# A 64-row half-width product and two row transfers in place of a full restoring product, in a two-layer attention kernel

## The chip, the cores and the metric

The kernel runs on one core of a Trainium2 chip. The metric is the time on the device for one execution, in microseconds (us), given as the median over runs. In what follows PE is TensorE (matmuls; PEld is its weight load), DVE is VectorE, ACT is ScalarE, POOL is GpSimd, and SP is the engine that only issues transfers. POOL issues transfers too, from a queue of its own.

## The reference, cut to what matters

Two residual attention layers run over four images of 32x32 tokens with 768 channels (12 heads of 64). The second layer, called layer 1 in the code, computes a depthwise 3x3 convolution of q, k and v, normalises each head, and adds q itself to what attention gives:

```python
q, k, v = (qkv[0], qkv[1], qkv[2])
q = layer_norm(dwconv3x3(q, w_pool_q), g_q, b_q)
k = layer_norm(dwconv3x3(k, w_pool_k), g_k, b_k)
v = layer_norm(dwconv3x3(v, w_pool_v), g_v, b_v)
ori_q = q
attn = jnp.einsum('bqc,bkc->bqk', qf * scale, kf)
attn = attn.reshape(B * nh, H, W, H, W) + rel_h[:, :, :, :, None] + rel_w[:, :, :, None, :]
attn = jax.nn.softmax(attn.reshape(B * nh, H * W, H * W), axis=-1)
o = attn @ vf
o = o.reshape(B * nh, H, W, hd) + ori_q
return o @ w_proj.T + b_proj
```

Layer 0 is plain attention with the same kind of relative-position terms. Each layer is preceded by a group norm.

## The kernel before, in words

**Stages and pairs.** The work is 8 stages of one image and one layer each, in the order (0,L0) (1,L0) (0,L1) (1,L1) (2,L0) (3,L0) (2,L1) (3,L1). A stage is six pairs of heads (`hp` 0 to 5), so there are 48 pairs, and 24 of them belong to layer 1. The 128 partitions hold two heads of 64 channels.

**Sixteen steps for a pair.** `attend` takes a pair in two halves of 512 queries (`c`), and each half in two groups of four key tiles. A group is four times [scores L804, relative-position term L806, exponential L811], then two steps in which other work is emitted, then the product with v (`av`, L828), then two more such steps. The relative-position term is a matmul of `bias` by a table of zeros and ones, `ones`, which is filled at the start from the input `picks` by two transfers and one ACT cast (L369).

**The order is written out by hand.** For PE, DVE, ACT and POOL the program order is the order in which the Python code emits instructions. `Pair.plan` lists what is prepared for a pair and at which step; step 0 is the start of the attention of the pair before it, so step -8 lies in the middle of the pair before that. In layer 1 the list has, among others: the product for q, k or v with its copy into a padded image (`padded(s, h)`: 24 matmul instructions `qkv`, then ACT L527), the nine taps of the convolution on DVE (L542, L544), `centre` (PE transposes `ln_c` L556 in two halves; for each half a DVE reduction L559 and a subtraction L560), `norm` (DVE L582), and `back` (PE transposes `ln_t` L591, then ACT L495 and L496 that write `q` and `q_t`). Work emitted at one step for different pairs follows in the order of the list `events`. Step 8 of one pair and step -8 of the next one coincide, so `centre(K)` of pair i, `padded(Q, 0)` of pair i+1 and, a step later, `back(Q, ...)` of pair i stand one behind another.

**Banks.** Products that are not scores take the PSUM banks of two places, left and right, in a fixed rotation, `behind_scores` being left, left, right, right and `behind_av` right, right, a small bank, left, left. A product waits for whoever used its bank last.

**The replaced channel.** In layer 1 channel 63 of each head's v is overwritten with ones (L584), so that rows 63 and 127 of `av` come out as the softmax's sums. `copy` (inside `attend`) brings `av` to SBUF as `weighed` (ACT L741), and two POOL transfers spread the two rows over all partitions: `z<-weighed` (L747) and `t<-z` (L748). A few steps later `sums` runs: `restore` (L751 to L755) multiplies the whole of `weighed` by a 128x128 matrix in the constants, `WHOLE`, which keeps 63 channels of a head and rebuilds the 64th as minus their sum (a normalised head sums to zero), in two products of 64 output rows each; ACT L755 copies the 128x512 result back. ACT L768, L776 and L777 then take the reciprocal of the sums, and at a later step `result` finishes on DVE: L784, L785, the division L788 (`inv<-weighed,inv`) and the addition of q (L789). Of the 48 halves of layer 1, 47 go this way. The very last half sums with `acc` and a product `z` instead, and restores afterwards.

**The end.** `project` multiplies the six pairs' outputs by the projection weights in seven products for a pair of output tiles. `put` adds product, bias and the residual `x` (L900), then a second term (L902), and stores (L903).

Of the kernel before, what the change touches and what calls it, by code (L numbers as in the profile page):

```python
# [9 lines left out]
F32 = mybir.dt.float32  # L10
F32R = mybir.dt.float32r
I32 = mybir.dt.int32
AF = mybir.ActivationFunctionType
ALU = mybir.AluOpType
# [3 lines left out]
P = 128  # L18
B = 4
S = 32  # L20
T = S * S
C = 768
NC = C // P
D = 64
HALF = T // 2
QC = 512
# [11 lines left out]
IDENT, GROUP, CENTRE, HEADS, ONES, WHOLE = 0, P, 2 * P, 3 * P, 3 * P + 2, 3 * P + 2 + D  # L38
# [7 lines left out]
def two_layers(ctx: ExitStack, tc: tile.TileContext, keep, x_in, wqkv, wproj, rels, windows, vrow, small, const, onehot, picks, out):  # L46
# [19 lines left out]
    nc = tc.nc  # L66
    pool = lambda name, bufs, **kw: ctx.enter_context(tc.tile_pool(name=name, bufs=bufs, **kw))
    fixed = pool("fixed", 1)
# [4 lines left out]
    one = pool("one", 1)  # L73
# [67 lines left out]
    cst = fixed.tile([P, NCONST], F32, tag="cst", name="cst")  # L141
# [5 lines left out]
    def col(c, lo=0, hi=P):  # L147
        return sm[lo:hi, c : c + 1]
# [15 lines left out]
    stages = [(b0 + k, layer) for b0 in range(0, B, 2) for layer in range(2) for k in range(2)]  # L164
# [53 lines left out]
    for i, (_, layer, hp) in enumerate(items):  # L218
        first = (i - 1) * 16 + shift(i)
# [142 lines left out]

    pbias = fixed.tile([P, NC], F32, tag="pbias", name="pbias")

    ones = fixed.tile([P, T], F32R, tag="ones", name="ones")
    plain = one.tile([P, T], F32, tag="whole", name="plain")
    for j in range(2):
        nc.sync.dma_start(plain[j * D : (j + 1) * D, :], picks)
    nc.scalar.copy(ones, plain)  # L369
# [5 lines left out]
    class Pair:  # L375
# [267 lines left out]
        def plan(self):  # L643

            Q, K, V = 0, 1, 2
            if not self.layer and not in_sevens(self.i):
                return [
                    (0, lambda: self.plain(Q, 0)),
                    (2, lambda: self.plain(Q, 1)),
                    (4, lambda: self.plain(K, 0)),  # L650
                    (5, lambda: self.positions(0)),
                    (6, lambda: self.plain(K, 1)),
                    (7, lambda: self.positions(1)),
                    (8, lambda: self.split()),
                    (8, lambda: self.plain_v(0)),
                    (10, lambda: self.plain_v(1)),
                ]
            if not self.layer:
                pieces = [
                    (0, lambda: self.sevens(Q, False)),  # L660
                    (2, lambda: self.sevens(Q, True)),
                ]

                first = 4 if shift(self.i) else 6
                pieces += [
                    (first, lambda: self.positions(0)),
                    (first + 2, lambda: self.positions(1)),
                    (first + 4, lambda: self.split()),
                ]
                if self.hp % 2 == 0:  # L670
                    pieces += [(8, lambda: self.sevens(V, False)), (10, lambda: self.sevens(V, True))]
                return [(r + shift(self.i), piece) for r, piece in pieces]


            late = self.hp in (0, NC // 2)
            pieces = [
                (-8, lambda: self.padded(Q, 0)),
                (-6, lambda: self.padded(Q, 1)),
                (-4, lambda: self.padded(K, 0)),
                (-2, lambda: self.padded(K, 1)),  # L680
                (2, lambda: self.padded(V, 0)),
                (4, lambda: self.padded(V, 1)),
                (3, lambda: self.centre(Q)),
                (4, lambda: self.square(Q)),
                (6, lambda: self.squares(Q)),
                (8 if late else 7, lambda: self.norm(Q)),
                (8, lambda: self.centre(K)),
                (9, lambda: self.back(Q, 0)),
                (9, lambda: self.back(Q, 1)),
                (10, lambda: self.square(K)),  # L690
                (11, lambda: self.squares(K)),
                (10, lambda: self.positions(0)),
                (11, lambda: self.positions(1)),
                (12, lambda: self.norm(K)),
                (11 if short(self.i) and self.hp == NC - 1 else 12, lambda: self.split()),
                (13, lambda: self.centre(V)),
                (14, lambda: self.back(K, 0)),
                (14, lambda: self.back(K, 1)),
                (14, lambda: self.square(V)),
                (15, lambda: self.squares(V)),  # L700
                (15, lambda: self.norm(V)),
            ]

            taps = (
                (Q, -4, (2, 2, 2, 2, 1)),
                (K, 2, (2, 2, 2, 2, 1)),
                (V, 8, (2, 2, 3, 2)),
            )
            for s, r, counts in taps:
                lo = 0  # L710
                for n in counts:
                    pieces.append((r, lambda s=s, lo=lo, n=n: self.taps(s, lo, lo + n)))
                    r, lo = r + 1, lo + n
            return pieces
# [4 lines left out]
    def attend(pair, os):  # L719


        q, k, bias = pair.q, pair.k, pair.bias
# [12 lines left out]
        for c in range(T // QC):  # L735
            cols = slice(c * QC, (c + 1) * QC)
# [14 lines left out]
            def restore(weighed):  # L751

                ps = small_bank("whole")
                halves(ps, cst[:, WHOLE : WHOLE + P], weighed)
                nc.scalar.copy(weighed, ps)  # L755

            def landed(*found):

                return found

            def sums(weighed, of, c=c, ones=by_ones[c]):

                at = 2 * (pair.i * (T // QC) + c)
                inv = work.tile([P, QC], F32, tag="inv", name="inv", bufs=1)
                if ones:
                    t = of
                    restore(weighed)
                    nc.scalar.activation(inv, t, AF.Copy, accum_out=seen[:, at : at + 1])  # L768
                else:
                    z = small_bank("z")  # L770
                    t = work.tile([P, QC], F32, tag="t", name="t", bufs=1)
                    for j, rows in enumerate(heads):
                        nc.tensor.matmul(z[rows, :], cst[:, ONES : ONES + D], of[:, j, :], start=True, stop=True)  # L773
                    nc.scalar.activation(t, z, AF.Copy, accum_out=seen[:, at : at + 1])

                nc.scalar.activation(inv, t, AF.Ln, bias=tiny)  # L776
                nc.scalar.activation(inv, inv, AF.Exp, scale=-1.0, accum_out=seen[:, at + 1 : at + 2])  # L777
                if pair.layer and not ones:
                    restore(weighed)
                return weighed, t, inv  # L780
# [17 lines left out]
            for g in range(0, NKT, 4):  # L798
                es = []
                for kt, place in zip(range(g, g + 4), (None, place_b, place_c, None)):  # L800
                    keys = slice(kt * P, (kt + 1) * P)
                    ps = place.pair("s") if place else ps_a.tile([P, 2, 512], F32, tag="a", name="s")
                    for j, rows in enumerate(heads):
                        nc.tensor.matmul(ps[:, j, :], k[rows, keys], q[rows, cols], start=True, stop=False)  # L804
                    for j, rows in enumerate(heads):
                        nc.tensor.matmul(  # L806
                            ps[:, j, :], ones[rows, keys], bias[c][rows, kt // 2, :],
                            start=False, stop=True,
                        )
                    e = work.tile([P, 2, QC], F32, tag="e", name="e", bufs=4)  # L810
                    nc.scalar.activation(e, ps, AF.Exp)  # L811
                    es.append(e)
# [12 lines left out]
                for t, e in enumerate(es):  # L825
                    kt = g + t
                    for j in range(2):
                        nc.tensor.matmul(  # L828
                            av[j * D : (j + 1) * D, :], pair.vt[:, kt, j * D : (j + 1) * D], e[:, j, :],
                            start=(kt == 0), stop=(kt == NKT - 1),  # L830
# [11 lines left out]
    def project(stage, os):  # L842
# [52 lines left out]
            nc.sync.dma_start(x, src[:, which, cols])  # L895
            return x

        def put(which, cols, x, ps, term=None):
            bias = pbias[:, which : which + 1] if layer else col(BIAS[0] + 18 + which)
            nc.vector.scalar_tensor_tensor(x, ps, bias, x, ALU.add, ALU.add)  # L900
            if term is not None:
                nc.vector.tensor_tensor(x, x, term, ALU.add)  # L902
            nc.sync.dma_start(dst[:, which, cols], x)  # L903

        add = lambda to, x, y, op=ALU.add: nc.vector.tensor_tensor(to, x, y, op)
# [34 lines left out]
        def three(pair):  # L940
            u, w = extra(9), extra(10)
            b3, b4 = bank("p1p6"), bank("p7")
            x11, x22 = get(2 * pair, first), get(2 * pair + 1, second)
            m(b3, pair, 4, lambda n: extra(n + 6))
            add(u, u, b3)
            m(b4, pair, 5, lambda n: os[n + 3][:, first])
            load(4 * pair + 4)
            put(2 * pair, first, x11, b4, u)
            m(b3, pair, 6, lambda n: os[n][:, second], more=True)
            load(4 * pair + 5)  # L950
            put(2 * pair + 1, second, x22, b3, w)

        def products():
            for pair in range(NC // 2):
# [320 lines left out]
def _laid_out(inp):  # L1275
# [38 lines left out]
    for i in range(S // 2):  # L1314
# [10 lines left out]
        "small": np.ascontiguousarray(np.concatenate(cols, axis=1)),  # L1325
        "const": const,
        "onehot": onehot.astype(np.float32),
        "picks": picks.reshape(D, T),
    }


# [15 lines left out]
```

## Time and profile before

| | |
|---|---|
| runs before | 3830.72, 3829.58, 3828.72 us; median 3829.58 |
| span of the profiled execution | 3830.7 us |
| mean granted TensorE clock | 0.999 |
| busy: PE / PEld | 3767.9 us (98%) / 1642.7 us |
| busy: DVE / ACT / POOL | 2468.2 (64%) / 1793.7 (47%) / 478.1 us (12%) |
| layer 1's taps on DVE, L544 | 758.2 us in 576, 1316 ns each |
| restoring products on PE, `whole<-weighed,cst` | 192 instructions, 4 for each of 48 |
| their copies on ACT, L755 | 28.1 us in 48, 586 ns each |

The table is from the summary page and from the groups of instructions. Busy times of different engines overlap and can't be added. An fp32 matmul of the program appears as two instructions. In the groups, the mean of a PE instruction is from its issue to its end and several are under way at once, so its busy total divided by its count tells more about its price than the mean. No time is given for the profiled execution beside its span; the span equals the first run shown, 3830.72 us, to the last digit that it has, and nothing measurable lies around it.

### The profile page before, as it was taken

How to read it: one execution, taken by the hardware profiler on the slowest of the kernel's cores; microseconds unless marked ns; L12 is line 12 of the kernel's file. 1: busy time of each engine (PE TensorE's matmuls, PEld its weight loads, DVE VectorE, ACT ScalarE, POOL GpSimd, SP SyncE). 2: the span in 40 equal slices, each digit the busy share in tenths (PEclk: the TensorE clock that was granted, in tenths of full speed). 3: DMA queues.
4: the chain of work that ended last, by engine and by line, in shares of the span. 5: the costliest groups of instructions: out<-in, count | busy, mean ns of one | idle time of the engine just before them, and what ended most of it. 6: DMA issues, size and time to landing. Idle time of an engine off the chain costs nothing.

```text
span 3830.7 us, 76084 instructions
## 1 busy us (share of the span) xinstructions
PE 3767.9 (98%) x32990; PEld 1642.7 (43%) x32990; DVE 2468.2 (64%) x3068; ACT 1793.7 (47%) x2573; POOL 478.1 (12%) x870
## 2 busy tenths in 40 slices
PE   8999999999999999999999999999999999999998
PEld 4535535533344443444535445355333444434442
DVE  2566454559678877688454564455686887867774
ACT  3455434545345553455534554254442555534552
POOL 0111100111111211111200010011111111111120
PEclk9999999999999999999999999999999999999999
DMA  4344452331431223311333122522124222142123
GB/s 155 103 120 118 131 151 83 101 79 42 124 94 48 64 51 98 119 47 48 83 114 121 52 76 61 178 58 75 44 55 141 66 60 55 48 124 62 46 57 100
DMA packets 211014, 330.62 MB, mean 86 GB/s; under 512 B 47570, under 2 KB 100562, under 8 KB 210672
## 3 DMA queue, kind: packets, MB, share of 16 engines
q1 hardware_dynamic: 122912, 212.26, 17.7%
q0 software_dynamic: 87760, 113.40, 12.4%
q8 instruction: 263, 4.31, 0.5%
q14 instruction: 79, 0.65, 0.1%
HBM read 184.62 MB, written 40.10 MB: 59 GB/s over the span
## 4 chain that ended last, share of the span: by engine, by line
PE 90%; DVE 6%; ACT 2%; DMA 1%; issue 1%; SPq 0%; POOL 0%; DVEq 0%; ACTq 0%
PE qkv L131 19%; PE s L804 17%; PE av L828 16%; PE m4m L131 5%; PE m3m L131 4%; PE m1m L131 4%; PE s L806 4%; PE p3p L131 3%; PE p4p L131 3%; PE p1p L131 3%; PE rel L613 3%; PE m L131 2%; PE ln_c L556 2%; DVE shared L544 1%; PE z L773 1%; PE whole L131 1%
## 5 line engine op out<-in xcount | busy, mean ns | idle before, releaser
L811 ACT ACTIVATE e<-s 128x1024 f32<-128x1024 f32 x768 | 775.0, 1024 | 423.2 <-PE s L806 392.8
L131 PE MATMUL qkv<-xn,wqkv_t 128*64 128x512 f32 x3648 | 814.4, 595 | 4.8 <-DVE gmean L334 2.6
L804 PE MATMUL s<-q,k 64*128 64x512 f32 x3072 | 807.1, 602 | 5.0 <-ACT e L811 4.1
L544 DVE SCALAR_TENSOR_TENSOR shared<-shared,sm 128x1056 f32<-128x1056 f32 x576 | 758.2, 1316 | 15.6
L806 PE MATMUL s<-bias,ones 64*128 64x512 f32 x1536 | 610.9, 788 | 1.0 <-DMA bias<-whole 1.0
L828 PE MATMUL av<-e,vt 128*64 128x512 f32 x2624 | 595.7, 596 | 0.0
L640 POOL DMA_DIRECT2D bias<-high x384 | 205.6, 556 | 2180.4 <-ACT high L629 1943.3
L131 PEld LDWEIGHTS qkv<-xn,wqkv_t 128*64 128x64 f32 x3648 | 251.3, 137 | 492.7 <-issue 482.8
L822 DVE TENSOR_TENSOR acc<-acc,e 128x1024 f32<-128x1024 f32 x294 | 360.2, 1225 | 114.0 <-ACT e L811 87.4
L804 PEld LDWEIGHTS s<-q,k 64*128 64x128 f32 x3072 | 279.4, 186 | 261.9 <-issue 210.7
L527 ACT ACTIVATE shared<-qkv,sm 128x512 f32<-128x512 f32 (+1 forms) x288 | 129.1, 501 | 500.0 <-PE qkv L131 500.0
L828 PEld LDWEIGHTS av<-e,vt 128*64 128x64 f32 x2624 | 181.3, 137 | 350.0 <-issue 315.4
L806 PEld LDWEIGHTS s<-bias,ones 64*128 64x128 f32 x1536 | 148.7, 187 | 184.2 <-issue 182.7
L640 POOL DMA_DIRECT2D bias<-whole x384 | 207.2, 571 | 55.7 <-DVE whole L630 46.7
L820 DVE TENSOR_TENSOR acc<-e 128x1024 f32<-128x1024 f32 x49 | 60.0, 1225 | 215.3 <-ACT e L811 206.7
L741 ACT COPY weighed<-av 128x512 f32<-128x512 f32 x96 | 56.3, 586 | 278.6 <-PE av L828 265.0
L559 DVE TENSOR_REDUCE mean<-ln_c 128x8 f32<-128x512 f32 x144 | 98.7, 686 | 114.5 <-PE ln_c L556 114.5
L613 PEld LDWEIGHTS rel<-q,rel 64*32 64x32 f32 x6144 | 111.8, 105 | 78.4 <-issue 73.5
L747 POOL DMA_DIRECT2D z<-weighed x47 | 27.2, 578 | 881.7 <-ACT weighed L741 476.3
L613 PE MATMUL rel<-q_t,rel 64*32 64x32 f32 x6144 | 123.4, 195 | 2.5 <-issue 2.5
L570 DVE TENSOR_REDUCE lnv<-shared 128x16 f32<-128x1024 f32 x72 | 87.5, 1216 | 58.2 <-ACT shared L566 58.2
L613 PE MATMUL rel<-q,rel 64*32 64x32 f32 x6144 | 122.4, 195 | 2.3 <-issue 2.3
(158 smaller groups left out, 4394.6 us busy)
## 6 DMA issues: line engine op xcount, KB each, us to landing
bias<-high POOLq DMA_DIRECT2D x384, 128.0 KB, 2.9
bias<-whole POOLq DMA_DIRECT2D x384, 128.0 KB, 3.0
wqkv_t<-in_wqkv SPq DMA_DIRECT2D x78, 384.0 KB, 3.2
wqkv_t<-mixed SPq DMA_DIRECT2D x66, 384.0 KB, 3.1
wproj_t<-mixed SPq DMA_DIRECT2D x48, 384.0 KB, 3.2
wqkv_t<-in_wqkv SPq DMA_DIRECT2D x66, 192.0 KB, 2.5
xn<-in_x SPq DMA_DIRECT2D x24, 512.0 KB, 8.8
x<-in_x SPq DMA_DIRECT2D x48, 256.0 KB, 3.3
```

What stands on the lines that cost most here:

```text
L131: nc.tensor.matmul(ps[lo : lo + D], a[:, lo : lo + D], b, start=start, stop=stop, **kw)
L527: nc.scalar.activation(self.pad[s][:, rows, there : there + src.shape[2]], src, AF.Identity, bias=col(self.column(s)))
L544: nc.vector.scalar_tensor_tensor(y, window, tap, y, ALU.mult, ALU.add)
L559: nc.vector.tensor_reduce(of, heads, AX.X, ALU.add)
L570: nc.vector.tensor_reduce(v, squared.rearrange("p (a d) -> p a d", d=D), AX.X, ALU.add)
L613: nc.tensor.matmul(ps[lo : lo + S, k * S : (k + 1) * S].rearrange("p (b c) -> p b c", b=2), rel[rows, 2 * self.layer + i, first : first + ...
L640: nc.gpsimd.dma_start(sets, some.unsqueeze(1).to_broadcast([D // 2, 2, QC]))
L804: nc.tensor.matmul(ps[:, j, :], k[rows, keys], q[rows, cols], start=True, stop=False)
L806: nc.tensor.matmul(ps[:, j, :], ones[rows, keys], bias[c][rows, kt // 2, :], start=False, stop=True,)
L811: nc.scalar.activation(e, ps, AF.Exp)
L822: nc.vector.tensor_tensor(acc, acc, e, ALU.add)
L828: nc.tensor.matmul(av[j * D : (j + 1) * D, :], pair.vt[:, kt, j * D : (j + 1) * D], e[:, j, :], start=(kt == 0), stop=(kt == NKT - 1),)
```

## The change

Four things are changed.

1. In the 47 halves that go by ones, `restore_last` replaces `restore`. Its weights are the odd columns of `WHOLE` (64 columns at a stride of two), whose last one of each 32 is the rebuilt channel of a head. Two products take 256 of the 512 columns each and land on the two halves of the partitions of one bank. ACT copies 128x256 to a new tile `last`, and two POOL transfers carry two rows of 256 values each into rows 63 and 127 of `weighed`.
2. `padded(Q, 0)` goes from step -8 to step -7, except for `hp` 1 and 4: the 24 instructions of the product, and its ACT copies, stand behind `back(Q, 0)` and `back(Q, 1)` of the pair before instead of ahead of them.
3. The table `ones` is 128x256 instead of 128x1024, and its input and load shrink with it; the four key tiles read the same two tiles of it in turn.
4. The last stage's last pair of output tiles adds the second term to `x` ahead of the product instead of behind it.

```diff
-    ones = fixed.tile([P, T], F32R, tag="ones", name="ones")
-    plain = one.tile([P, T], F32, tag="whole", name="plain")
+    ones = fixed.tile([P, 2 * P], F32R, tag="ones", name="ones")
+    plain = one.tile([P, 2 * P], F32, tag="whole", name="plain")
...
+            early_late = self.hp in (1, NC // 2 + 1)
             pieces = [
-                (-8, lambda: self.padded(Q, 0)),
+                (-8 if early_late else -7, lambda: self.padded(Q, 0)),
...
+            def restore_last(weighed):
+
+                ps = small_bank("last")
+                odd = cst[:, WHOLE + 1 : WHOLE + P : 2]
+                for h in range(2):
+                    nc.tensor.matmul(
+                        ps[h * D : (h + 1) * D, : QC // 2], odd, weighed[:, h * (QC // 2) : (h + 1) * (QC // 2)],
+                        start=True, stop=True,
+                    )
+                last = one.tile([P, QC // 2], F32, tag="last", name="last")
+                nc.scalar.copy(last, ps[:, : QC // 2])
+                for h in range(2):
+                    rows = last[h * D + D // 2 - 1 : (h + 1) * D : D // 2, :]
+                    nc.gpsimd.dma_start(weighed[D - 1 :: D, h * (QC // 2) : (h + 1) * (QC // 2)], rows)
...
                 if ones:
                     t = of
-                    restore(weighed)
+                    restore_last(weighed)
...
-                            ps[:, j, :], ones[rows, keys], bias[c][rows, kt // 2, :],
+                            ps[:, j, :], ones[rows, kt % 2 * P : (kt % 2 + 1) * P], bias[c][rows, kt // 2, :],
...
-        def put(which, cols, x, ps, term=None):
+        def put(which, cols, x, ps, term=None, term_first=False):
...
+            if term is not None and term_first:
+                add(x, x, term)
             nc.vector.scalar_tensor_tensor(x, ps, bias, x, ALU.add, ALU.add)
-            if term is not None:
-                nc.vector.tensor_tensor(x, x, term, ALU.add)
+            if term is not None and not term_first:
+                add(x, x, term)
...
+            last = stage == stages[-1] and pair == NC // 2 - 1
-            put(2 * pair, first, x11, b4, u)
+            put(2 * pair, first, x11, b4, u, last)
-            put(2 * pair + 1, second, x22, b3, w)
+            put(2 * pair + 1, second, x22, b3, w, last)
...
-        "picks": picks.reshape(D, T),
+        "picks": np.ascontiguousarray(picks.reshape(D, T)[:, : 2 * P]),
```

## The prediction

> **What bounds the kernel now.** I read the summary page first.
>
> ```profile
> PE 3767.9 (98%) x32990; PEld 1642.7 (43%) x32990; DVE 2468.2 (64%) x3068; ACT 1793.7 (47%) x2573; POOL 478.1 (12%) x870
> PE 90%; DVE 6%; ACT 2%; DMA 1%; issue 1%; SPq 0%; POOL 0%; DVEq 0%; ACTq 0%
> ```
>
> The first line is busy time by engine, the second the chain that ended last, by engine. PE is busy for 98% and is 90% of the chain; all its gaps make 63 us. So a PE instruction that goes is worth its time if nothing late stands just behind it. Next the groups of instructions, for the operations that the change touches:
>
> ```profile
> L131 PE MATMUL whole<-weighed,cst 128*64 128x512 f32 x192 | 50.0, 599 | 2.0 <-ACT t L774 2.0
> L131 PE MATMUL m3m<-wqkv_t,xn 128*64 128x128 f32 x1056 | 62.0, 273 | 0.0
> L755 ACT COPY weighed<-whole 128x512 f32<-128x512 f32 x48 | 28.1, 586 | 169.3 <-PE whole L131 167.4 <-issue 1.9
> L747 POOL DMA_DIRECT2D z<-weighed x47 | 27.2, 578 | 881.7 <-ACT weighed L741 476.3 <-ACT ln_ln L153 309.6 <-ACT ln_gn L153 95.8
> ```
>
> Here the restoring product is 192 instructions, four for each half. The second row is another product with 64 columns of weights that moves 128 columns. On the timeline, four `whole` instructions take 0.858 us from start to the next instruction's start where a product follows: 0.2145 each.
>
> For the moved product I read PE's and DVE's timelines, at one of its two places where the norm comes late:
>
> ```profile
> 1451.54 1.09 PE L556 MATMUL ln_c<-cst,shared 128*128 128x128 f32 x8
> 1452.56 5.37 PE L131 MATMUL qkv<-xn,wqkv_t 128*64 128x512 f32 x24
> 1457.86 1.09 PE L591 MATMUL ln_t<-cst,shared 128*128 128x128 f32 x8
> ```
>
> ```profile
> 1451.95 1.22 DVE L582 TENSOR_TENSOR shared<-shared,r_ln 128x1024 f32<-128x1024 f32 x1
> 1453.09 0.68 DVE L559 TENSOR_REDUCE mean<-ln_c 128x8 f32<-128x512 f32 x1
> 1453.81 0.69 DVE L560 SCALAR_TENSOR_TENSOR shared<-mean,ln_c 128x512 f32<-128x512 f32 x1
> ```
>
> The columns are start and duration. `ln_t` reads what L582 writes (it ends at 1453.17), so today the product's 5.3 us cover that wait. For the start I read the chain of its first 40 us:
>
> ```profile
> 8.20 9.70 DMA plain<-in_picks
> ...
> 17.99 1.04 ACT ones L369
> 19.03 0.11 ACT ln_gn L153
> ```
>
> The table's load and cast stand ahead of the group norm on the path to the first product.
>
> **What the Trainium skill says.** "TensorE: Matmul & The Clock Gate", section "Wait — 56ns, not 53.3ns?", gives columns / 2.4 GHz plus 2.5 ns for a matmul; the trace agrees (0.2145 us at 512; 62.0/1056 = 0.0587 at 128). "SBUF — State Buffer", section "Specifications (TRN2)", has cachelines of 16 bytes that want two hits for full bandwidth; weights at a stride of two fp32 have two. No row of before shows strided weights. "DMA: Bandwidth & Descriptors", "Anatomy of one DMA — SWDGE (gpsimd) path", prices a POOL transfer at about 2.0 us fixed; the trace has a median of 1.7 us from issue to landing for `z<-weighed`, 4 KB. "SBUF — State Buffer", "SBUF: two separate sides", warns that some DVE operations lock POOL out of writing descriptors; this trace suggests it (POOL L748 starts up to 2.75 us late behind a DVE L886).
>
> **The change part by part.**
>
> *The shorter product.* A new instruction moves 256 columns. Between 0.0587 at 128 and 0.2145 at 512, the line gives 0.111, so four take 0.443 and each restore gives back 0.858 - 0.443 = 0.415 us. 47 of them: -19.5. Two of the 47 (at 1813.9 and 3701.5) lie ahead of `rel` stretches where PE stalls by over 2 us anyway; I count those lost, with the like smaller cases: +0.8. Sum **-18.7**, between -17.5 (more of it lost in gaps) and -20.4. If strided weights loaded at half speed, four loads at twice the 0.056 us that 128-column products sustain would take 0.112 each, beside matmuls of 0.111: no cost.
>
> *The copy.* 128x256 for 128x512 saves about 0.25 us on ACT, which is idle ahead of it (169.3 us over 48): nothing, since neither ACT nor what follows it there is on the path, except at the end (below).
>
> *The two transfers.* Each of 47 restores adds two POOL issues at about 0.57 us (54 us on an engine 12% busy) and one wait: L788 on DVE now waits for their landing. From L755's end to L788's start the trace has 8.5 us at the least in the ordinary halves, 11.8 and 17.9 in others. Needed: 2 x 0.57 + 1.7 = 2.9 us. POOL's own `z`, `t` and bias issues then lie elsewhere; the nearest bias ones start over 3 us later. The transfers take the POOL queue's turn ahead of the bias transfers by 1.1 us, and those wait far longer for ACT's `high`. Behind L788 stand the taps, and behind these `ln_c` on PE, but with 5 us to spare the cost is 0. If the cover went, DVE's gaps of 2.9 to 6.6 us ahead of K's centre would take the first of it.
>
> *The end.* In the last pair's first half, L755 ends at 3754.09 and L788 starts at 3757.71: 3.6 us of cover against 2.9, and L788 is on the path there (L788, L741, L774, then PE after a gap of 1.96). The shorter product and copy bring up to -0.7; a late landing up to +1. I take **0**.
>
> *The moved product.* In 14 places it changes its order on PE (in the first layer-1 pair the order is the same). Before: `ln_c` 1.02, `qkv` 5.30, `ln_t` 1.02, no gap. After: `ln_c`, `ln_t`, `qkv`. Two waits appear. `ln_t` needs L582, which ends before `ln_t` can start in 12 places and 0.6 us after in two. And by the rotation of the banks the product takes the bank of the first half of `ln_c`, so it waits for the first L560, 2.11 us after `ln_c` starts (0.15 more to PE), when `ln_t` has ended at 1.9 to 2.0: 0.3 us. In rows without a product between them, `ln_c` plus `ln_t` take 1.90 instead of 2.04, so net I take 0.1 for 12 places (0 to 0.3), 0.95 for two (to 1.2): 1.2 + 1.9 = **+3.1**, between -1 and +6. Below nothing because ACT's `q` and `q_t` come 5 us earlier; but `q_t` ends 0.96 us ahead of the `rel` that reads it, and after 0.43 less of `restore` still 0.5 ahead, so I see no PE gap that this closes. What is late next is the product's copy, L527, and the taps come four steps later.
>
> *The narrow table.* 64 KB instead of 256 KB twice, and a cast of 0.35 instead of 1.04 us. The path then passes to the group's statistics, whose last DVE operation ends at 17.74; the logarithm could start about 17.9 instead of 19.03. **-1.15** (-1.5 to 0). The weights that the 1536 `bias` matmuls read from the table keep their shape: 0.
>
> *The last tiles.* The final L900 and L902 (0.75 and 0.69) follow the last product. With the addition put first, it must wait for its `x`, issued at 3820.23 and landed at 3823.3, just ahead of the product's end at 3823.5: **-0.2** (-0.7 to 0).
>
> Sum: -18.7 + 0 + 3.1 - 1.15 - 0.2 = -17.0 on 3830.7, 3813.7. The three runs' median stands 1.1 below the span: **3812.6**. All bounds together give 3806 to 3819.
>
> **The rivals.**
>
> *Waits take the gain's place (chance 0.12).* PE's queue is in order; if the moved product waited for both halves of `ln_c` (3.43 us after its start) or if DVE ran later than today, it would stall 1.5 us in 14 places, +21 instead of +3: 3830, no change. For it: `PE ln_t` already waits 6.1 us for L560 in seven places. Against: today's DVE order is kept, and the bank is the first half's. Half of it would give 3821.
>
> *The transfers land late (0.05), the other side.* The place is L788: the trace shows POOL held up by DVE, and the taps fill DVE at 1316 ns each, so descriptors could wait. Up to 8.5 us nothing happens; the next 2.9 us go into DVE's gap; from about 11.4 us each further us costs 47 on PE. It turns slower at 11.8 us; at 12.4 the bill is +47 - 17 = +30: 3860. Against: `z<-weighed` never took above 4.2 us to land, under the same taps.
>
> *The product doesn't get shorter (0.06).* If a strided load took 0.2 us, four times today's, it would replace the matmul as the limit and the first term would go: 3830.7 - 1.1 + 3.1 - 1.35, about 3831. Against: the two hits in a line above.
>
> **How the numbers follow.** The sum as worked out has 0.77. What a measurement here can tell from no change is 0.2%, 7.7 us. Its own range is 3806 to 3819; to hold 8 in 10 I stretch it to 3821 for a half-eaten gain. Faster by over 0.2%: 0.77 and some half of the first rival: 0.84. Within: the rest of it and the third, 0.11. Slower: 0.05.
>
> **What would show it.** Right: a row `last<-weighed,cst` of 188 instructions at some 21 us busy; PE busy down by 19 to 21 us; `ln_c`, `ln_t`, `qkv` with gaps of 0.3 us ahead of `qkv`; L788 (now L804) never released by a DMA except perhaps in the last pair; the first product about 1.1 us earlier. Wrong: waits of DVE for `weighed` by DMA, gaps over 1 us ahead of the moved product, or a `last` row with over 30 us.

## The result, and the profile after

The changed kernel takes 3815.74 us (median of 4 runs, 3814.61 to 3816.65) against 3830.15 before: a ratio of 0.9959, interval 0.9945 to 0.9973. Two repeats beside other experiments gave 3814.64 against 3831.85 (0.9956, 0.9943 to 0.9970) and 3814.63 against 3831.83 (0.9953, 0.9939 to 0.9967). So the change saves between 14 and 17 us, 0.4 to 0.5%; -17.0 was forecast, and 3812.6 for the median, 3.1 below the first of these results. The profiled execution's span went from 3830.7 to 3814.6, by 16.1.

One reading ahead of the change was wrong at the outset: something does lie around the span. The profiled execution of after lasted 3816.61 us with a span of 3814.6, so some 2.0 us. A span of before of 3830.7 then stands for an estimated 3832.7, which is above its median and not equal to its first run. Changes of spans are therefore compared with each other below, and medians with medians.

The summary page of after, busy time by engine:

```profile
PE 3749.5 (98%) x32990; PEld 1656.7 (43%) x32990; DVE 2467.1 (65%) x3068; ACT 1786.5 (47%) x2573; POOL 529.1 (14%) x964
```

PE lost 18.4 us of busy time and is still the bound; POOL gained 51 us for 94 more instructions. The groups of instructions of after, for the new operations (busy time, mean ns of one, then idle time before them):

```profile
L763 PE MATMUL last<-weighed,cst 128*64 128x256 f32 x188 | 28.9, 381 | 0.0
L768 ACT COPY last<-last 128x256 f32<-128x256 f32 x47 | 17.5, 372 | 175.8 <-PE last L763 175.8
L771 POOL DMA_DIRECT2D weighed<-last x94 | 50.7, 541 | 679.6 <-ACT last L768 638.6 <-DVE shared L544 38.1 <-issue 2.9
```

In the busy total of a PE group each run of instructions counts its last one to its modelled end, after the next product has begun, so the price is read from starts: on the timeline, four `last` instructions take 0.431 us to the next product's start, where four `whole` took 0.858. One place on PE's timeline, of before and then of after:

```profile
1205.65 1.03 PE L131 MATMUL whole<-weighed,cst 128*64 128x512 f32 x4
1206.51 5.32 PE L131 MATMUL qkv<-xn,wqkv_t 128*64 128x512 f32 x24
```

```profile
1204.75 0.60 PE L763 MATMUL last<-weighed,cst 128*64 128x256 f32 x4
1205.18 5.32 PE L131 MATMUL qkv<-xn,wqkv_t 128*64 128x512 f32 x24
```

The saving is 0.427 for each restore.

Where the time went is seen by subtracting, for the same exponential on ACT, its start in the two timelines. The difference is nearly a staircase: it falls by 0.36 to 0.45, mostly 0.43, for one restore after the other through layer 1, stage after stage, with few exceptions. The main ones are the start (-0.37 at the first exponential), a rise by 1.7 near 915 us, a rise by 0.84 above the expected step near 1450 and 3340 us, a rise by 2.9 near 1815 us, and the end, where it goes from -14.0 to -16.1. The experiments were chosen for these.

PE's timeline at one of the two late places of the move, to be held against the lines of the same place before:

```profile
1447.64 1.09 PE L556 MATMUL ln_c<-cst,shared 128*128 128x128 f32 x8
1449.41 1.06 PE L591 MATMUL ln_t<-cst,shared 128*128 128x128 f32 x8 [0.67 <-DVE shared L582]
1450.68 5.37 PE L131 MATMUL qkv<-xn,wqkv_t 128*64 128x512 f32 x24 [0.21 <-PE ln_t L591]
```

and at one of the twelve ordinary ones:

```profile
1082.93 1.09 PE L556 MATMUL ln_c<-cst,shared 128*128 128x128 f32 x8
1083.86 1.04 PE L591 MATMUL ln_t<-cst,shared 128*128 128x128 f32 x8
1085.18 5.37 PE L131 MATMUL qkv<-xn,wqkv_t 128*64 128x512 f32 x24 [0.28 <-DVE shared L560]
```

The bracket is PE's idle time ahead and what ended it. The two forecast waits are there: `ln_t` for the norm L582 (0.67), and the product for the first L560 (0.28). From `ln_c` to the instruction behind the three groups the ordinary places take 7.38 to 7.43 us, where they took 7.34 to 7.35; the late ones take 8.21.

At the start, ACT's timeline has the cast of the table at 16.36, 0.41 us long, while the statistics still run, instead of between them and the logarithm. But the last DVE statistics of `xn` now start at 15.02 instead of 14.22, waiting for their load, so the first product starts at 20.68 instead of 21.05: 0.37 earlier. At the end, DVE's timeline has

```profile
3807.40 0.69 DVE L923 TENSOR_TENSOR x<-x,os_sums 128x512 f32<-128x512 f32 x1 [1.91 <-DMA x<-mid]
3808.20 0.75 DVE L918 SCALAR_TENSOR_TENSOR x<-p1p,pbias,x 128x512 f32<-128x512 f32 x1
```

so the last addition (L923, moved ahead) waits for the load of its `x`. From the start of the last product's group to the end of DVE it is 4.55 us against 4.28 before. Of the kernels below, e13 has the new order too and takes 4.25, and e10 has the old one and takes 4.63, so no difference between the orders is shown.

The rise near 1815 us is the one that nothing in the prediction named. ACT's timeline of after there:

```profile
1808.14 0.37 ACT L768 COPY last<-last 128x256 f32<-128x256 f32 x1 [0.85 <-PE last L763]
1811.12 0.63 ACT L784 ACTIVATE inv<-t 128x512 f32<-128x512 f32 x1 [2.61 <-DMA t<-z]
...
1814.21 0.56 ACT L618 COPY whole<-rel 64x512 f32<-64x512 f32 x1
1814.78 1.01 ACT L619 COPY whole<-rel 64x512 f32<-64x512 f32 x1
```

and of before:

```profile
1815.01 0.59 ACT L755 COPY weighed<-whole 128x512 f32<-128x512 f32 x1 [1.28 <-PE whole L131]
1815.49 0.63 ACT L768 ACTIVATE inv<-t 128x512 f32<-128x512 f32 x1
```

Before, the activation followed the copy at once. Now it waits 2.61 us for `t`, the sums spread by the two older transfers, and the copies of the relative positions stand behind it in ACT's order. PE waits 1.76 us between the two relative products, where it waited 2.49 before, and then 2.63 us more for those copies (L619), which it did not before. Then comes a stretch at a lower clock (the columns are the window, its length, busy time by engine, the granted PE clock, DMA share and GB/s):

```profile
914.00:918.00 4.00, 4.00 (x12) 1.12 (x10) 3.89 (x4) 1.62 (x2) 0.94 (x2) 0.57 0.67 170
1819.00:1826.00 7.00, 6.04 (x20) 3.05 (x22) 6.72 (x12) 3.71 (x6) 7.00 (x15) 0.52 0.83 193
```

The first line is the rise near 915: behind a gap of 1.88 us, which before has too, PE runs at half clock for 3.4 us and loses 1.7. Of the drop from -14.0 to -16.1 at the end, 1.7 is a stretch at half clock that before has near 3760 us and after has not at the same work, and 0.43 is the last restore.

### The profile page after: what moved, and what is told of

Read it like the earlier page. It is cut to its first block, busy times and chain, and to the rows that moved or that the text cites. A ratio compares the mean times of both kernels' runs of the same rounds, so it can differ in the third digit from the quotient of the medians.

```text
span 3814.6 us, 76313 instructions
## 1 busy us (share of the span) xinstructions
PE 3749.5 (98%) x32990; PEld 1656.7 (43%) x32990; DVE 2467.1 (65%) x3068; ACT 1786.5 (47%) x2573; POOL 529.1 (14%) x964
## 5 line engine op out<-in xcount | busy, mean ns | idle before, releaser
L771 POOL DMA_DIRECT2D weighed<-last x94 | 50.7, 541 | 679.6 <-ACT last L768 638.6
L412 DVE TENSOR_TENSOR shared<-shared,m3m 128x512 f32<-128x512 f32 x66 | 45.3, 687 | 119.9 <-PE m3m L131 119.8
```

## The experiments

My theory after the result: all of the gain is the shorter restore, 0.427 us in 46 of 47 halves; the move costs 0.85 in two places; the table and the tail are worth little; and the one lost place is the late `t`. Rivals: the move pays for something that shows only with the shorter restore; the loss near 1815 is chance; the added transfers cost by themselves.

| kernel | median us | before beside it | ratio (interval) |
|---|---|---|---|
| e2, move only | 3833.65 | 3831.82 | 1.0006 (0.9998 to 1.0014) |
| e4, table and tail only | 3830.50 | 3831.82 | 0.9996 (0.9988 to 1.0004) |
| e3, all but the move | 3812.45 | 3831.82 | 0.9949 (0.9935 to 0.9962) |
| e5, fewer moves, old tail | 3812.12 | 3831.82 | 0.9950 (0.9936 to 0.9963) |
| e9, the change again | 3814.64 | 3831.85 | 0.9956 (0.9943 to 0.9970) |
| e6, e5 with sums one slot later | 3823.14 | 3831.85 | 0.9977 (0.9969 to 0.9985) |
| e7, rows land later (8) | 3821.20 | 3831.85 | 0.9972 (0.9961 to 0.9982) |
| e8, rows land later (20) | 3903.37 | 3831.85 | 1.0184 (1.0168 to 1.0200) |
| e10, restore and table only | 3813.33 | 3831.83 | 0.9949 (0.9935 to 0.9962) |
| e11, e10 with the sums behind `rel` | 3809.77 | 3831.83 | 0.9941 (0.9927 to 0.9955) |
| e12, e10 behind both `rel` | 3822.04 | 3831.83 | 0.9973 (0.9963 to 0.9984) |
| e13, the change a third time | 3814.63 | 3831.83 | 0.9953 (0.9939 to 0.9967) |

The kernels ran on three chips, each beside before; the medians of before agree to 0.03 us.

**The parts by themselves.** e2 is before with the move:

```diff
+            early_late = self.hp in (1, NC // 2 + 1)
-                (-8, lambda: self.padded(Q, 0)),
+                (-8 if early_late else -7, lambda: self.padded(Q, 0)),
```

> The kernel before with the move of q's first half alone. Theory (move nearly free): ln_t now stands 0.3 us ahead of the moved product in 12 of 14 places and costs nothing net there; two places (stages 4 and 8, pair hp 0's second half) cost 0.85 us each, so +1.7 us, about 3831. The step as predicted: +3.1 us (between -1 and +6). Rival (the move is what gains, by q and q_t being ready 5 us earlier): below before by 1 us or more.

It came out 1.8 above before, within the interval of no difference. The timelines tell more: against before, the exponentials step by +0.85 at the two late places and by under 0.1 at the twelve others (a step of 1.7 near 2810 is a stretch of half clock again: a granted clock of 0.82 and 0.75 over the two halves of 2808 to 2816). From `ln_c` to the instruction behind the three groups the twelve cost 0.03 to 0.07 each, 0.5 together. The move gains nothing that shows and costs some 2.2.

e4 has the narrow table and the tail's order:

```diff
-    ones = fixed.tile([P, T], F32R, tag="ones", name="ones")
+    ones = fixed.tile([P, 2 * P], F32R, tag="ones", name="ones")
...
+            if term is not None and term_first:
+                add(x, x, term)
```

> The kernel before with the narrow table and the tail's order alone. Theory from the two profiles: the cast leaves the chain but the last load of xn lands later, so the first product comes 0.3 to 1.1 us earlier; the tail's addition waits for its x and costs 0.3 us. Together -0.8 to 0, about 3829. As predicted: -1.35 us. Rival (narrow rows make the table's load no faster and delay xn by as much): 0 at the start in this kernel too.

1.3 below before, again within no difference. Its first exponential comes 0.61 earlier than in the one profile of before. In the other profiles with the narrow table it came between 1.06 earlier and, in e6, 0.71 later, and 0.61 later in e2, which has the wide one. The cast leaves the path, but a gain is not told apart from the varying arrival of `xn`.

e3 is the changed kernel with the first diff undone, e10 the same with the tail's order undone as well:

> The changed kernel with the move undone: shorter restore, narrow table, tail. Theory (47 restores give 0.43 us each on PE, all but one or two kept): about -19.5 - 0.4 + 0.3, so 3810 us, some 2 below the changed kernel where neither loses time to the clock. Rival (the move pays for something that only shows once the restore is shorter, such as q_t in time for the relative positions): at or above the changed kernel, 3814 or more, with waits of PE for q_t.

> The kernel before with the shorter restore and the narrow table alone (the restore's new tile does not fit without it): no move, old tail. Theory: the whole gain is here, 46 x 0.43 - 1 for the lost one, so about 3811 to 3812, equal to the kernels with the move. Rival (move and tail help a little): 3 us above them, 3814 or more.

Both lie below the changed kernel, by 2.2 and 1.3 us against the repeats, and waits of PE for `q_t` appear in neither. The runs of e3 don't overlap with the repeats' (3811.03 to 3813.02 against 3813.41 to 3816.18); those of e10 do (3810.14 to 3816.0). The rival in which the move pays falls. (The restore is not tried without the narrow table, since its new tile finds no room beside the wide one.)

e5 keeps the move but for the two late places, and the old tail:

```diff
-            early_late = self.hp in (1, NC // 2 + 1)
+            early_late = self.hp in (1, NC // 2 + 1) or self.hp == 2 and self.b % 2
...
-            last = stage == stages[-1] and pair == NC // 2 - 1
+            last = False
```

> The changed kernel with the two late places of the move (hp 2 of the stages of images 1 and 3) left in the old order and the tail's order undone. Theory: 2 x 0.85 + 0.3, so 2.0 us below the changed kernel, about 3812 at the median, 3810 where the clock takes nothing. Rival (the losses seen in its profile come with the added transfers or the shorter restore, not with the move): no different from the changed kernel, with PE at half clock in the same two places (near 914 and 1820 us).

2.5 below the two repeats of the changed kernel. Against e9 its exponentials step by -0.84 at just those two places. The rival's second half held in part: half clock near 1815 is in e5 too (0.83 over 1808 to 1818), so it does not need the late moves. It is in e4 as well, at 1819, with the full restore, so it is no mark of the shorter one either.

**Is the loss near 1815 chance?** e9 is the change again.

> The changed kernel once more, beside the others. Theory: about 3814 to 3816, some 2 to 3 us above the kernel without the late moves and the tail's order, with an ACT wait for t<-z of 2 us or more near 1810 us and PE at half clock behind it. Rival (the wait was chance of one execution): no such wait here.

The ACT wait for `t<-z` is there (2.3 us in two places, 1.9 the longest), the half clock isn't, and the step is +1.7 above the expected one instead of +3.3. The same wait is in e3, e5, e10 and e13, 1.9 to 2.3 us at the longest, and not in before, e2 and e4, which keep the full restore. So the wait is systematic and the half clock behind it comes and goes.

POOL's timeline has the reason. At this place it shows, in after and then in e7, the kernel with eight more transfers for each restore that is described below:

```profile
1798.55 0.54 POOL L748 DMA_DIRECT2D z<-weighed  x1 [18.62 <-ACT weighed L742]
1803.06 0.81 POOL L749 DMA_DIRECT2D t<-z  x1 [3.97 <-issue]
```

```profile
1798.18 0.54 POOL L748 DMA_DIRECT2D z<-weighed  x1 [14.31 <-ACT weighed L742]
1800.34 0.81 POOL L749 DMA_DIRECT2D t<-z  x1 [1.62 <-DVE r_ln L160]
```

In both, `z` lands 1.6 us after its issue, and `t` could follow. In after it follows 2.9 us later, in e7 0.55. From `z` to `t` it is 4.5 us in every kernel with just the 94 added transfers, 3.0 to 3.1 in before, e2 and e4, and 2.16 in e7 and e8, which have the shorter restore and more transfers still. In e7 and e8 ACT does not wait for `t` here, and the exponentials of e7 fall by the usual 0.43 against before. So the shorter restore keeps its gain at this place when `t` is issued in time, and what takes the gain is the pause of POOL.

The pause goes by the number of transfers that POOL has issued. In the nine kernels with just the 94 added ones it falls ahead of the `t` of the same three halves, the 13th, 21st and 42nd of 47, and lasts 2.8 to 3.1 us from the landing of `z`; in before, e2 and e4 it falls ahead of the 5th and 35th, in e7 ahead of the 3rd. In after the transfers behind a pause are POOL's 250th, 354th, 450th, 571st, 692nd, 797th and 902nd. The added transfers shifted it to a place where `t` has no room: in this form the rival that they cost by themselves holds. What POOL does in the pause no view names.

e6 gives `t` more time by one slot of the other work:

```diff
-                    n_parts = 2 if short(pair.i) and (pair.hp, c) in ((NC - 2, 1), (NC - 1, 0)) else 1
+                    n_parts = 2 if short(pair.i) and (pair.hp, c) in ((NC - 2, 0), (NC - 2, 1), (NC - 1, 0)) else 1
```

> The kernel with the fewer moves and the old tail, and the sums of hp 4's first half in the stages before layer 0 taken one slot later (so its restore and reciprocal come two steps on, at two places, near 1810 and 3690 us). Theory: ACT no longer waits for t<-z there, the relative positions' copies behind it come on time, PE has no gap long enough to lose its clock; 1.5 to 3 us below the kernel without that (3812), about 3810. Rival (PE idles there for another reason, the copies of the relative positions themselves): the gap and the half clock stay, and nothing is gained.

11 us slower than e5 by the medians, 6 by the spans of the profiled executions; its runs spread from 3816.72 to 3826.02. The wait went (0.3 us is left of it), and the exponentials gain 2.3 and 1.0 where they should. A step later they lose 3.9 and 4.7. PE's waits of e6:

```profile
PE s L820 <- ACT k L504: 10.0, 2, 5.1
```

(total, times, longest). `k` of the next pair now comes behind the sums' work, and the scores wait for it. The wait was moved, for a worse one.

e11 and e12 leave the slot and change the order within it, on top of e10:

```diff
                 other_work(behind_av)
-                more()
+                behind = short(pair.i) and pair.hp == NC - 2 and (c, g) == (1, 0)
+                if not behind:
+                    more()
...
                 yield
+                if behind:
+                    more()
                 yield
```

(e12 has the second addition behind the second `yield`.)

> As the kernel with restore and table alone, but in hp 4's first half of the stages before layer 0 (two places, near 1810 and 3690 us) the sums' step, restore and reciprocals, is emitted behind the first relative-position product instead of ahead of it. Theory: the copies of the relative positions no longer stand behind ACT's wait for t<-z; of the gap of 2.0 to 2.4 us between the two relative products some 2 us go in each place: -2 to -4, about 3808 to 3810. Rival (the wait moves to the second product's copies and the scores behind them): 0 to -1.

3.6 below e10 and 4.9 below the changed kernel, whose runs it doesn't touch (3809.23 to 3811.36 against 3813.97 to 3815.23): the lowest median of the study. PE's waits of e10, then of e11:

```profile
PE rel L613 <- issue: 4.8, 2, 2.4
```

```profile
PE rel L613 <- issue: 2.7, 2, 1.6
```

The first relative product's copies no longer stand behind `t`, and the gap to the second product shrinks by 2.1 us over the two places. The exponentials step by -2.5 and -0.85, and give back +0.8 and +1.6 at the next pair. So 0.9 of the 4.4 us between the two spans is at the two places; stretches at half clock that e10 has near 2800 and 3741 and e11 has not make up most of the rest. That the order itself gains the whole 3.6 of the medians is not shown.

> The same with the step behind both relative-position products and the split. Theory: -3 to -5, as t has landed by then and ACT has nothing to wait for; 3807 to 3809. Rival (the next exponentials then stand behind the reciprocals on ACT, 2.3 us, and DVE's result comes late, as in the kernel with the sums one slot later, where the scores waited 5 us for k): slower than the first variant by 2 us or more.

12 us slower than e11, but not for the reason given. The waits of e12:

```profile
DVE inv L803 <- DMA weighed<-last: 12.9, 2, 6.5
PE ln_t L591 <- DVE shared L582: 12.6, 2, 6.4
```

Emitted behind the split, the two row transfers stand behind its sixteen `bias` transfers on POOL. DVE's division waits 6.5 us for the rows, the norm L582 waits behind it on DVE, and PE's `ln_t` waits for the norm, 6.4 us. This is the prediction's slow rival, in two places, with nearly each microsecond of DVE's wait turned into one of PE's.

**How late may the rows land?** e7 and e8 put transfers that nobody reads ahead of the two row transfers:

```diff
+                junk = dram.tile([8, 2, QC // 2], F32, tag="junk", name="junk", bufs=2)
+                for n in range(8):
+                    nc.gpsimd.dma_start(junk[n], last[D // 2 - 1 : D : D // 2, :])
                 for h in range(2):
```

> The changed kernel with eight more small transfers on POOL's queue ahead of the two that carry the rows (writes of two rows to a scratch in HBM, read by nobody). The rows land some 7.2 us after ACT's copy instead of 2.9. Theory: 7.8 us of room in the tightest ordinary halves, so nothing in 45 of 47; the last pair's two halves have 2.9 us of room and pay about 4.4 us each where DVE's division is on the path: +4 to +9 us. Rival (added POOL traffic itself costs, by other transfers' lateness or the HBM): more than +10, spread over layer 1.

> The same with twenty more: the rows land some 13.7 us after the copy. The prediction's price: free up to 11.4 us, then 47 us for each further us, so about +108 and the tail's 10 to 20. Theory now: only the 16 or so halves with 7.8 to 8.9 us of room overrun DVE's gap (by some 2 to 3 us each, +30 to +50), those with 11.3 us wait 2.4 us within the gap for nothing, and the tail pays 10 to 20: +40 to +70. Rival (DVE is not near the path at all): the tail's 10 to 20 alone.

e7 is 6.6 above e9, inside the theory's 4 to 9. DVE's waits of e7, then of e8:

```profile
DVE inv L807 <- DMA weighed<-last: 12.4, 4, 3.3
```

```profile
DVE inv L807 <- DMA weighed<-last: 146.6, 39, 9.7
```

In e7 four halves wait at all. Against e9 the exponentials rise by 3.2 in the last pair; ahead of it they rise by 1.7 in one stretch at half clock and fall by 1.7 near 1815, where `t` is on time. e8 is 88.7 above e9, between the two forecasts of it: 39 of 47 halves wait, for 146.6 us in all. The prediction's price (108 and the tail) was too high: it charged all 47 halves alike, while the eight with 17 to 18 us of room don't wait at all, and those with 12.0 wait some 1.3. The theory of the moment (40 to 70) was too low, since these last do pay (about 1.2 each on the exponentials where it can be followed), and since neither forecast had the clock: the mean granted clock is 0.989 in e8 and 0.998 in e9, which times their spans (3901.4 and 3811.4) is an estimated 35 of the 88.7 us. That the path goes by DVE is clear: `PE ln_t L591 <- DVE shared L560` rises from 6.1 us in after to 25.4 in e8.

> The changed kernel beside the others, on one chip. Theory: 2 to 3 us above the kernel with restore and table alone: two late places of the move 1.7, the tail 0.3, and now and then a stretch of half clock. Rival (no difference): within 1 us.

1.3 above e10, between theory and rival and with runs that overlap, and 2.5 above e5. The two places of the move show at +0.84 each in its timeline against e10.

## Why the prediction was right, point by point

The forecast of -17.0 stands against -16.1 in the spans and -14.4, -17.2 and -17.2 in the medians. The likeliest case was the one that happened. That the sum came so close is in part luck: the terms as measured in after add to -16.7 + 2.2 - 0.4 + 0.3 = -14.6, and stretches at half clock and small steps, for which the prediction has no term, make the rest. (Its outer bounds add to 3805.3 to 3819.1, a little more than the 3806 to 3819 that it gives.)

*The shorter product* was put at -18.7. The price of a strided, half-wide instruction by the line between 128 and 512 columns was 0.111; it measured 0.431 / 4 = 0.108, so the strided weights cost nothing that shows. The row `last` has 28.9 us busy instead of some 21, near the 30 that was to be a sign of being wrong, but the starts decide (a busy total counts the overlapping ends too), and PE's busy time fell by 18.4, just under the 19 to 21 forecast. Of the two halves written off because PE stalls behind them, one kept its gain (near 3690, where the gap shrank from 2.27 to 1.92 us) and the other lost it and 1.3 (e9) to 2.9 us (after) more: the term should have been -19.6 for 46 halves and +1.3 to +2.9 for the lost one, so -18.3 to -16.7. **The step that was wrong** is the reason for that loss: the stall of PE behind a restore takes nothing by itself, as e7 shows, where the half near 1815 keeps its gain.

*The copy and the transfers* at 0: right for the rows. No wait of DVE for them is in after, and the median from issue to landing is 1.7 us as assumed. In the last pair they land 2.4 us behind the copy, with 3.6 of room. What the term left out is what the added transfers do to the others on POOL's queue: they shifted POOL's pause to the `t` near 1815, and that half lost 0.43 and 1.3 to 2.9 us. The prediction's sign that DVE holds POOL up was a misreading: the `t` that starts 2.75 us behind a DVE L886 waits for `z`, which lands 2.74 us after its issue. And in the pause of before near 3272 us DVE has nothing to do.

*The moved product* was put at +3.1; the timelines of after and e2 give +2.2. The two waits, their releasers and their sizes were as worked out (0.28 for 0.3, 0.67 for 0.6); the mis-sized term is the twelve ordinary places, 0.03 to 0.07 instead of 0.1 each. The gain side, q ready earlier, brought nothing, as argued.

*The table* was put at -1.15; -0.37 here, and -1.06 to +0.71 over the kernels. The cast left the path, but the load of `xn` that ends the path came 0.8 us later in after, and such variation the sum had not.

*The tail* at -0.2 was +0.27 here: the load of `x` did not land "just ahead of the product's end" but just behind it, 3807.3 for an end near 3807.2. Over the kernels nothing is shown either way. The bound stopped at 0 for no good reason.

*The rivals.* Waits in the gain's place did appear in a small form, through POOL and ACT and not through PE's moved product. The late landing of the rows was not in after, but e8 and e12 show its mechanism. That the product doesn't get shorter is refuted by the starts.

## What to carry to other kernels

When PE is the bound, a shorter PE instruction is worth its full time at each place but those where something else on another in-order engine arrives just in time; look there for the transfer with the least room before counting the gain. Added transfers can delay older ones on the same queue without standing ahead of them: here one `t` of 47 came late because a pause of POOL had moved, and with more transfers still the pause was elsewhere. A step that is cheap for the engine that waits can be dear for what is queued behind it: the same reciprocals behind one product gave the lowest median here, behind two products and a burst of transfers they cost 12 us more than that. And when rows are fetched by transfers instead of being computed, measure the room (here 8.5 to 18.1 us from the copy's end to the division, 3.6 in the last pair): inside it they are free, and beyond it PE's gaps bring stretches at half clock on top of the wait.

## What the runs showed of the hardware that was not expected

PE's granted clock halves for stretches of 3.4 us, some of them twice or three times as long, at spots that differ between executions of the same kernel, mostly behind a gap of some 2 us, and each 3.4 us costs about 1.7 us where PE has work. Apart from the last microseconds, the profile of before has two, near 3760 and 3777 us, that of after four, near 914, 1819 (twice as long), 3693 and 3761, and that of e9 two, near 3690 and 3759. Two profiles that differ by a few microseconds are therefore compared place by place, with these stretches set aside; their sum over a span is as large as the smaller terms of this change.

POOL pauses for 1.5 to 4 us at fixed counts of its transfers. The counts are the same in all profiles with the same transfers (after, e9 and e13, and e3 and e10 as well), and change when transfers are added. Where a pause falls ahead of a transfer that is waited for, its lateness looks like a wait for whatever ended last on another engine: of the three `t` behind a pause in after, the profile puts two down to nothing and one to a DVE instruction.
